# Depthwise convolutions on quarters of the array, and other rules for placing pieces, in a chain of four layers

## The chip, the cores and the metric

The kernel runs on one core of one Trainium2 chip. The metric is device time in microseconds (us), the median of several executions; lower is better. The engines are TensorE (PE, matrix products, with its weight loads shown as PEld), VectorE (DVE), ScalarE (ACT), GpSimd (POOL) and SyncE (SP), whose queue issues the transfers (DMA).

## What is computed

The input is x, 16 images of 192 channels and 32x32 pixels, in f32. Four layers follow each other: an mLSTM block with a 3x3 convolution and a batch norm over all images (layer 0); two attention blocks over channels with depthwise 3x3 convolutions (layer 1, of which the output needs the second attention with the first one's weights); a selective scan in four directions (layer 2); and a graph layer with sparse neighbours, a projection and a Gelu (layer 3). What the change touches is in layers 1 and 2:

```python
def dwconv3x3(x, w):
    return lax.conv_general_dilated(x, w, window_strides=(1, 1), padding='SAME', feature_group_count=x.shape[1], ...)
...
qkv = dwconv3x3(conv1x1(x, w_qkv), w_qkv_dw)
...
kvf = dwconv3x3(conv1x1(out, w_kv), w_kv_dw)
...
def step(h, xs_t):
    d_t, u_t, B_t, C_t = xs_t
    dA = jnp.exp(d_t[..., None] * A)
    h = h * dA + (d_t * u_t)[..., None] * B_t[:, :, None, :]
    y = jnp.einsum('bkdn,bkn->bkd', h, C_t)
    return (h, y)
```

In layer 2 an image has 384 inner channels, 16 states a channel, four directions and 1024 steps. Its depthwise convolution has 384 channels; those of layer 1 that the output needs have 384 (q and k), 192 (v) and 192 (the second v).

## The kernel before

Layer 0 runs over all images first and leaves its result in device memory. The rest is the class `LayersB`. Each image has three parts: `prepare` (layer 1 and the entry of layer 2), the scans of layer 2, and `complete` (the end of layer 2 and layer 3). While image b is scanned, `prepare(b + 1)` and `complete(b - 1)` run beside it as background streams. The first preparation and the last completion stand alone.

**The scans.** An image has 4 directions x 24 groups of 16 channels x 2 blocks of 8 states, 192 units (`UNITS`). One unit u is: `decay` (line 1830, ACT: h = exp(dl x A), 128x1024, into one of two PSUM buffers), `inputs` (line 1837, POOL: xs = du x bb, three buffers, two units ahead), `scan` (line 1844, DVE, in place in h), `outputs` (line 1849, DVE: hc = h x cb, three buffers), `sums` (line 1882, PE: four matmuls that add hc into the accumulator acc) and, each eighth unit, `collect` (line 1892, ACT copies acc to y). `fetch` loads dl, du, bb and cb on SP's queue. In directions 1 and 3 the sums read hc across (128 bytes from element to element).

**The projections.** `front(k)` makes dl and du of a direction, in six halves of 512 columns: `steps` (a matmul with dtw), `ends` (ACT: Abs and Relu), `logs` (ACT: Exp and Ln), `park` (POOL: dlh and duh, then two stores). `project` and `keep` do the same for the states, for two directions at once. Each piece has its unit written out by hand, with lags of 0, 1, 2 and 4 units.

**The background streams.** `prepare` and `complete` are generators. They yield the engine that their next piece needs. `scans` is a planner that runs when the program is built: it keeps a clock for each engine, adds to it what `Metered` puts down for each background instruction (`RATES`) and what a unit needs (`OWN`, `SLOT`), and lets a stream advance in a unit where `fits` says that the engine's clock lies less than `OVER` past the unit's end. `ALLOW` meters PE and DVE besides: 2.7 and 0.3 us of background work a unit. The instructions of each engine then stand in the order in which the planner issued them, and each engine takes its own in that order.

**Convolutions.** `conv` has ten calls an image: two for v and two for the second v (96 channels), three for q and k, three for layer 2 (128 channels). It takes the image padded to 34x34 from one of two pads, in two halves of 16 rows (512 columns), and for each half adds nine matmuls in one PSUM bank, each with a diagonal p x p weight matrix for its tap (from line 1140). An ACT copy takes each half away. `taps` loads the diagonal matrices from device memory, three taps a load; in the first image it makes them on DVE and stores them, and there DVE computes the second half of each convolution.

**PSUM.** Two tiles h of two banks each, acc of one, and one bank each for `prepare` ("bp"), `complete` ("bc") and `front` ("bf").

**Tables of ACT.** Gelu, Tanh and Ln with Exp need different function tables. `ln_exp` loads the one with Ln; a load is an instruction on ACT's queue. After each group of Gelu pieces the streams call `ln_exp`.

Nearly all background instructions have line 800, since `Metered` issues them.

Of the kernel before, what the change touches and what calls it, by code (L numbers as in the profile page):

```python
# [41 lines left out]
class Ctx:  # L42


    def __init__(self, tc, cpool, I):
        self.tc, self.nc, self.I = tc, tc.nc, I
        self.ordered = False
        self.has_ln = False
        nc = self.nc
        self.ident = cpool.tile([128, 128], F32, name="ident")  # L50
        nc.sync.dma_start(self.ident, I["c_ident"])
        self.blk6 = cpool.tile([P6, P6], F32, name="blk6")
        nc.sync.dma_start(self.blk6, I["c_blk6"])
        self.eps5 = cpool.tile([128, 1], F32, name="eps5")
        nc.vector.memset(self.eps5, 1e-5)
        self.one = cpool.tile([128, 1], F32, name="one")
        nc.vector.memset(self.one, 1.0)
        self.on192 = cpool.tile([P6, P6], F32, name="on192")
        nc.vector.memset(self.on192, 1.0 / C)
        self.on384 = cpool.tile([128, 128], F32, name="on384")  # L60
        nc.vector.memset(self.on384, 1.0 / INNER)
        self.ones = cpool.tile([128, 128], F32, name="ones")
        nc.vector.memset(self.ones, 1.0)

    def ln_exp(self):

        if self.ordered and self.has_ln:
            return
        self.has_ln = True
        if self.ordered:  # L70
            self.spent["ACT"] += TABLE
        i = self.nc.scalar.preload_act_table_set("natural_log_exp_and_others")
        if not self.ordered:
            self.tc.keep_in_program_order(i)
# [696 lines left out]
SLOT = 3.55  # L771
EARLY = 1.3
OWN = {"POOL": 2.36, "SUMS": 0.6, "START": 0.9, "DECAY": 1.1, "COLLECT": 0.57}
ENGINES = ("PE", "ACT", "POOL", "DVE")
ALLOW = {"PE": 2.7, "DVE": 0.3}
OVER = {"PE": 2.5, "ACT": 1.0, "POOL": 2.5}
LEAST = {"PE": 1.0, "ACT": 0.6, "POOL": 0.8}
# [3 lines left out]

class Metered:


    RATES = {"ACT": (0.07, 0.00105), "POOL": (0.1, 0.0022), "DVE": (0.08, 0.00105), "PE": (0.06, 0.0017)}
    LEAST = {"ACT": 0.2, "POOL": 0.2, "DVE": 0.12, "PE": 0.4}

# [3 lines left out]
    def __getattr__(self, op):  # L791
        f = getattr(self.engine, op)

        def issue(out, *args, **kw):
            base, each = self.RATES[self.name]
            self.spent[self.name] += max(self.LEAST[self.name], base + each * math.prod(out.shape[1:]))
            if op == "activation" and args[1] in (AF.Tanh, AF.Gelu):
                self.spent["ACT"] += TABLE * self.cx.has_ln
                self.cx.has_ln = False
            return f(out, *args, **kw)  # L800

        return issue
# [12 lines left out]
class Stream:  # L815
# [9 lines left out]
    def step(self):  # L825
        self.engine, lag, *mark = next(self.pieces, (None, 0))
        self.ready = self.at + lag
        self.piped = "piped" in mark

# [11 lines left out]
class LayersB:  # L841
# [10 lines left out]
    def mm(self):  # L852

        if self.bank is None:
            self.turn = (self.turn + 1) % 3
            tag = ("bp", "bc", "bf")[self.turn]
        else:
            tag = self.bank
        return self.mmp.tile([128, HL], F32, tag=tag, name="mm")

# [25 lines left out]
    def run(self):  # L886
        tc, NB = self.tc, self.NB
        self.bank, self.turn = None, 0
        with ExitStack() as ctx:
# [11 lines left out]
            self.parked = self.fetched = self.slots = self.scanned = self.read = 0  # L901

# [11 lines left out]
            with tc.manual_schedule():  # L914
                self.before, self.after = Stream(self.all(self.complete), "bc"), Stream(self.all(self.prepare), "bp")
                for b in range(NB):
# [6 lines left out]
    def setup(self):  # L923
# [3 lines left out]
        self.dqd = dp.tile([6, 128, 9, 128], F32, name="dqd")  # L927
        self.dvd = dp.tile([2, 2, P6, 9, P6], F32, name="dvd")
# [168 lines left out]
    def taps(self, p, src, w, first):  # L1097


        d = [self.slot("dg", [p, 3, p], "dg", 3) for _ in range(3)]  # L1100
        tv = None
# [3 lines left out]
        for t in range(3):  # L1105
            three = slice(3 * t, 3 * t + 3)
            if first:
                self.nc.vector.tensor_mul(
                    d[t], self.cx.ident[0:p, 0:p].unsqueeze(1).to_broadcast([p, 3, p]),
                    tv[:, three].unsqueeze(2).to_broadcast([p, 3, p]),  # L1110
                )
                self.nc.sync.dma_start(src[:, three, :], d[t])
            else:
                self.nc.sync.dma_start(d[t], src[:, three, :])
        return d, tv

    def conv(self, out, i, p, taps):


        nc = self.be  # L1120
        d, tv = taps
        for hf in range(2):
            if hf and tv is not None:
                yield "DVE", 0
                o = rows(out[:, half(hf)])
                for t in range(9):
                    v = self.pads[i][0:p, 16 + t // 3 : 32 + t // 3, t % 3 : t % 3 + W]
                    if t == 0:
                        nc.vector.tensor_scalar(o, v, tv[:, 0:1], None, op0=ALU.mult)
                    else:  # L1130
                        nc.vector.scalar_tensor_tensor(
                            o, v, tv[:, t : t + 1], o, op0=ALU.mult, op1=ALU.add
                        )
                continue
            yield "PE", 0
            ps = self.mm()[0:p, :]
            for t in range(9):
                if t in (2, 4, 6):
                    yield "PE", 0
                nc.tensor.matmul(  # L1140
                    ps, lhsT=d[t // 3][:, t % 3, :],
                    rhs=self.pads[i][0:p, 16 * hf + t // 3 : 16 * hf + t // 3 + 16, t % 3 : t % 3 + W],
                    start=(t == 0), stop=(t == 8),
                )
            yield "ACT", 0
            nc.scalar.copy(out[:, half(hf)], ps)

    def prepare(self, b):
# [193 lines left out]
        for g in range(3):  # L1342
            yield "ACT", 0
            nc.scalar.activation(xx[:, g, :], xg[:, g, :], AF.Gelu, bias=self.dw2b[:, g : g + 1])
        cx.ln_exp()
# [7 lines left out]
        for gs in ((0, 1), (2,)):  # L1353
# [10 lines left out]
            for g, z in zip(gs, zs):  # L1364
                yield "ACT", 0
                nc.scalar.activation(z, z, AF.Gelu)
                nc.sync.dma_start(self.zd[one(b), g].rearrange("o p l -> p (o l)"), z)
            cx.ln_exp()
# [5 lines left out]
    def complete(self, b):  # L1374
# [176 lines left out]
        for hf in range(2):  # L1551
# [57 lines left out]
            yield "ACT", 0  # L1609
            nc.scalar.activation(fin, fin, AF.Gelu)  # L1610
            cx.ln_exp()
# [22 lines left out]
    def scans(self, b, more, carry):  # L1634
# [4 lines left out]
        ahead = {}  # L1639
        for d in range(K + more):  # L1640
            for at, piece in self.front(d % K):
                if d % K or (at < 0) == (d > 0):
                    ahead.setdefault(d * DIR_UNITS + at, []).append(piece)
        for t in range(UNITS):
# [3 lines left out]
            for s in (self.before, self.after):  # L1648
                while s.engine == "ACT" and self.fits(s, now + EARLY - OVER["ACT"]):
                    self.advance(s)  # L1650
            if more or t + 1 < UNITS:
                self.decay((t + 1) % UNITS)
                clock["ACT"] += OWN["DECAY"]
# [4 lines left out]
            self.outputs(t)  # L1658
            clock["DVE"] += SLOT
            end = now + SLOT  # L1660
            if t > 0 or carry:
                self.sums((t - 1) % UNITS)
                self.collect((t - 1) % UNITS)
            self.fetch(t, more)
            self.bank = "bf"
            was = dict(self.spent)
            for piece in ahead.pop(t, ()):
                piece()
            for e in ENGINES:
                clock[e] += self.spent[e] - was[e]  # L1670
            for e in ALLOW:
                have[e] = min(have[e], 0.0) + ALLOW[e] - self.spent[e] + was[e]
            if more and t == FETCH:
                while self.parked < b + 2:
                    self.advance(self.after)
                self.fetch_xx()
            if t == UNITS - DIR_UNITS:
                while self.read < b:
                    self.advance(self.before)
            if t == 2:  # L1680
                self.scanned = b
            streams = (self.before, self.after)[:: 1 if t % 2 else -1]
# [6 lines left out]
        if not more:  # L1689
            while self.before.engine:  # L1690
                self.advance(self.before)
# [3 lines left out]
    def fits(self, s, end):  # L1695

        if not s.open(self.slots) or s.engine == "SP":
            return s.engine == "SP" and s.open(self.slots)
        at = self.clock[s.engine]
        if s.engine != "DVE":  # L1700
            end += OVER[s.engine]
        wait = s.inputs()
        if wait > at and (s.engine == "DVE" or wait + LEAST[s.engine] > end):
            return False
        return at < end + 0.1 and self.have.get(s.engine, 1.0) > 0.0

    def advance(self, stream):
        self.bank = stream.bank
        stream.at = self.slots
        was, wait = dict(self.spent), stream.inputs()  # L1710
        stream.step()
        for e in ENGINES:
# [7 lines left out]
    def begin(self):  # L1720

        for at, piece in self.front(0):
            if at < 0:
                piece()
# [12 lines left out]
    def front(self, k):  # L1737


# [48 lines left out]
        out = []  # L1788
        if k % 2 == 0:
            for hf in range(2):  # L1790
                at = -24 + 2 * hf
                out += [(at, lambda hf=hf: project(hf)), (at + 1, lambda hf=hf: keep(hf))]
        for n, at in enumerate((-18, -12, -6, 0, 6, 12)):
            for lag, f in ((0, steps), (1, ends), (2, logs), (4, park)):
                out.append((at + lag, lambda f=f, n=n: f(n // 2, n % 2)))
        return out
# [31 lines left out]
    def decay(self, u):  # L1828
        n, blk = divmod(u, BLOCKS)
        self.nc.scalar.activation(  # L1830
# [8 lines left out]
    def scan(self, u):  # L1839

        h, x = self.h[u % 2], self.xs[u % 3]
        if u // DIR_UNITS >= 2:
            h, x = h[:, ::-1], x[:, ::-1]
        self.nc.vector.tensor_tensor_scan(h, h, x, 0.0, op0=ALU.mult, op1=ALU.add)  # L1844
# [14 lines left out]
    def sums(self, u):  # L1859
# [5 lines left out]
        self.clock["PE"] += OWN["SUMS"]  # L1865
# [132 lines left out]
```

## Time and profile before

| | us |
|---|---|
| three runs | 15,191.56, 15,242.16, 15,250.05 |
| median | 15,242.16 |
| the profiled execution | 15,228.48 |
| its span, first to last instruction | 15,226.7 |

Busy time in the span, from the page:

| engine | busy us | share |
|---|---|---|
| PE | 12,507.7 | 82% |
| DVE | 12,530.6 | 82% |
| ACT | 7,798.3 | 51% |
| POOL | 10,305.3 | 68% |

The shares are means over stages with different limits. Up to about 3,090 us the span is layer 0, in which PE is busy 95% of the time and DVE under 50%. From there on the first preparation takes some 210 us, the scans of 16 images run from 3,300 to 15,079, and the last completion ends at 15,227.

The costliest groups have one line each in the page: instructions by line, engine and operation, what they write and read, the count, then busy us and mean ns of one. A scan (line 1844) takes 2,288 ns and its product (line 1849) 1,225 ns, 3,072 of each; a decay 1,116 ns; an xs 2,365 ns. A matmul in f32 leaves two records in the trace, one after the other. In the lists of waits a line names the waiting engine and tile, what ended the wait, and then the us in total, the times and the longest.

### The profile page before, as it was taken

To read this page: it belongs to the slowest core of one execution; us is meant where nothing else is said; L and a number is where in the kernel's file an instruction comes from. 1 tells how busy PE (TensorE), PEld (TensorE's weight loads), DVE (VectorE), ACT (ScalarE), POOL (GpSimd) and SP (SyncE) were. 2 spreads that over 40 slices of the span, in tenths; PEclk is the share of its full clock that TensorE was granted. 3 is DMA by queue.
4 is the path that set the end of the run, shared out by engine and by line. 5 is a ranking of instruction groups with operands and counts; after the bars stand their busy time and mean duration, and the time that the engine had idled before them with its cause. 6 is when DMAs were issued, how large, how long until landed. Compare 5 with 4: busy or idle time off the path is not lost. (4 is left out here: it accounts for less than half of the span.)

```text
span 15226.7 us, 183204 instructions
## 1 busy us (share of the span) xinstructions
PE 12507.7 (82%) x65856; PEld 4757.9 (31%) x65856; DVE 12530.6 (82%) x10115; ACT 7798.3 (51%) x10376; POOL 10305.3 (68%) x6314
## 2 busy tenths in 40 slices
PE   8999999978787778788887878788887888787655
PEld 4444444422232222222222222222222222222212
DVE  4444444459899999999999899999999999989997
ACT  3333333334555556465646565655555555555554
POOL 2222222227687878787878787878888787878785
PEclk9999999978888888888888888888888878888766
DMA  1000000047778787878777778777777787777775
GB/s 29 15 15 15 15 15 15 15 109 192 202 195 212 188 209 193 209 196 204 195 201 200 195 199 199 202 196 204 196 199 201 203 197 204 193 205 195 198 181 128
DMA packets 884772, 2412.01 MB, mean 158 GB/s; under 512 B 146672, under 2 KB 266944, under 8 KB 876224
## 3 DMA queue, kind: packets, MB, share of 16 engines
q1 hardware_dynamic: 871168, 2397.50, 62.2%
q8 instruction: 532, 8.72, 0.3%
q10 hardware_dynamic: 12736, 3.04, 0.1%
q14 instruction: 336, 2.75, 0.1%
HBM read 2019.10 MB, written 364.30 MB: 157 GB/s over the span
## 5 line engine op out<-in xcount | busy, mean ns | idle before, releaser
L1837 POOL TENSOR_TENSOR xs<-du,bb 128x1024 f32<-128x1024 f32 x3072 | 7236.2, 2365 | 1967.3 <-DVE h L1844 1511.0
L1844 DVE TENSOR_TENSOR_SCAN h<-h,xs 128x1024 f32<-128x1024 f32 x3072 | 7028.1, 2288 | 440.3 <-ACT h L1830 391.4
L1830 ACT ACTIVATE h<-dl,A 128x1024 f32<-128x1024 f32 x3072 | 3424.6, 1116 | 3605.1 <-DVE hc L1849 3066.4
L1882 PE MATMUL acc<-hc,sel 128*32 128x256 f32 x24576 | 2741.8, 527 | 1651.5 <-DVE hc L1849 1640.5
L1849 DVE TENSOR_TENSOR hc<-h,cb 128x1024 f32<-128x1024 f32 x3072 | 3761.9, 1225 | 363.3 <-PE acc L1882 53.0
L800 PE MATMUL mm<-pad,dg 128*128 128x512 f32 (+1 forms) x5580 | 2791.1, 637 | 152.1 <-DMA dg<-dqd 39.0
L627 POOL TENSOR_TENSOR D<-D,mask 128x256 f32<-128x256 f32 x768 | 543.4, 740 | 2100.1 <-DVE D L624 2100.1
L1882 PEld LDWEIGHTS acc<-hc,sel 128*32 128x32 f32 x24576 | 549.8, 118 | 3958.7 <-DVE hc L1849 2717.5
L800 PEld LDWEIGHTS mm<-pad,dg 128*128 128x128 f32 (+1 forms) x5580 | 970.4, 187 | 1682.2 <-issue 1399.8
L800 PE MATMUL mm<-x,wgt 96*128 96x512 f32 (+1 forms) x1664 | 1067.3, 775 | 148.9 <-ACT o L800 43.2
L800 POOL TENSOR_TENSOR t<-x 96x768 f32<-96x768 f32 (+4 forms) x510 | 650.8, 1298 | 79.5 <-ACT x L800 47.8
L800 PE MATMUL mm<-d,xT 128*96 128x256 f32 x2048 | 588.5, 428 | 15.8 <-POOL d L800 13.3
L800 PE MATMUL mm<-xd,dtw 12*128 12x512 f32 x768 | 559.1, 815 | 8.0 <-ACT z L800 8.0
L800 POOL TENSOR_TENSOR duh<-dlh,xx 128x512 f32<-128x512 f32 x384 | 538.3, 1402 | 30.1
L800 POOL TENSOR_TENSOR dlh<-dlh,e 128x512 f32<-128x512 f32 x384 | 488.4, 1272 | 103.7 <-ACT e L800 101.8
L800 PEld LDWEIGHTS mm<-x,wgt 96*128 96x128 f32 (+1 forms) x1664 | 335.4, 223 | 697.1 <-issue 339.9
L391 PE MATMUL pc<-ypad,w_c 128*64 128x512 f32 (+1 forms) x1152 | 480.2, 664 | 74.4 <-PEq L751 41.6
L1892 ACT COPY y<-acc 128x512 f32<-128x512 f32 x384 | 224.6, 585 | 543.3 <-PE acc L1882 539.2
L624 DVE SCALAR_TENSOR_TENSOR D<-D,s 128x256 f32<-128x256 f32 x768 | 271.6, 415 | 255.3 <-ACT D L620 255.3
L1870 PE MATMUL acc<-y,ident 128*128 128x512 f32 x576 | 387.7, 761 | 84.9 <-ACT y L1892 84.9
L800 PEld LDWEIGHTS mm<-d,xT 128*96 128x96 f32 x2048 | 340.2, 179 | 321.2 <-issue 131.6
L620 ACT ACTIVATE D<-s 128x256 f32<-128x256 f32 x768 | 233.3, 389 | 337.9 <-PE s L613 332.4
(321 smaller groups left out, 14230.1 us busy)
## 6 DMA issues: line engine op xcount, KB each, us to landing
dl<-dld SPq DMA_DIRECT2D x1536, 512.0 KB
du<-dud SPq DMA_DIRECT2D x1536, 512.0 KB
dld<-dlh SPq DMA_DIRECT2D x384, 256.0 KB
dud<-duh SPq DMA_DIRECT2D x384, 256.0 KB
bb<-xdr SPq DMA_DIRECT2D x128, 512.0 KB
cb<-xdr SPq DMA_DIRECT2D x128, 512.0 KB
dg<-dqd SPq DMA_DIRECT2D x270, 192.0 KB
zd<-z SPq DMA_DIRECT2D x48, 512.0 KB
```

Source lines behind the costliest of these rows:

```text
L391: nc.tensor.matmul(p[r, :], lhsT=w_, rhs=v, start=(n == 0), stop=(n == 14))
L620: nc.scalar.activation(d, S[j][:, two], AF.Exp)
L624: nc.vector.scalar_tensor_tensor(d, d, 2.0, S[j][:, 2 * CH :], op0=ALU.min, op1=ALU.mult)
L627: nc.gpsimd.tensor_mul(d, d, mask)
L800: return f(out, *args, **kw)
L1830: self.nc.scalar.activation(self.h[u % 2], self.dl[n % 2], AF.Exp, scale=self.A[:, blk, n : n + 1])
L1837: self.nc.gpsimd.tensor_mul(self.xs[u % 3], self.du[n % 3], self.turn_of(self.bb, n // GROUPS, blk))
L1844: self.nc.vector.tensor_tensor_scan(h, h, x, 0.0, op0=ALU.mult, op1=ALU.add)
L1849: self.nc.vector.tensor_mul(self.hc[u % 3], self.h[u % 2], self.turn_of(self.cb, k, at % BLOCKS))
L1870: nc.tensor.matmul(acc, lhsT=self.cx.ident, rhs=self.y[:, g, half(pair)], start=True, stop=False)
L1882: nc.tensor.matmul(self.acc[rows4(q), q4(s)], lhsT=self.sel[:, m, :], rhs=part(q), start=False, stop=(s + m + blk == 3),)
L1892: self.nc.scalar.copy(y, self.acc)
```

## The change

It has five parts.

1. Convolutions: each tap is four matmuls. Channels 0 to 63 and the rest are two row blocks, the two halves of the image two column blocks; a row block has its own PSUM bank ("bf" is taken besides the stream's own, `mm2`). The weights are 64 columns wide, one load for nine taps, two buffers. For 96 channels the second block is 32 rows by 32 columns. The planner adds `TAP` for each tap. Four ACT copies of 64x512 (or 32x512) take the result away. The DVE path of the first image goes.
2. Projections: `front` becomes a generator, `fronts`, and a third stream with the first claim. Its pieces have an earliest unit and a latest one, at which `force` issues them.
3. A lock: who is to use "bf" says "take" and "give"; the other waits between.
4. Gelu pieces are marked; they are issued where they end by the plan 1.2 us ahead of the unit's end, and the next decay loads the table with Ln back.
5. The planner's figures change. PE isn't metered any more, background DVE pieces may stand between a scan and its product, and PE is held to 1.0 us past the unit's end ahead of each eighth unit. A function `pooled`, which is False for every unit, has branches of its own; none of them is taken.

```diff
-SLOT = 3.55
+SCAN, PRODUCT = 2.29, 1.34
 EARLY = 1.3
-OWN = {"POOL": 2.36, "SUMS": 0.6, "START": 0.9, "DECAY": 1.1, "COLLECT": 0.57}
+OWN = {"POOL": 2.37, "SUMS": 0.8, "TURNED": 1.05, "START": 1.25, "DECAY": 1.12, "COLLECT": 0.59}
+TAP = 1.2
-ALLOW = {"PE": 2.7, "DVE": 0.3}
+ALLOW = {"DVE": 0.45}
 OVER = {"PE": 2.5, "ACT": 1.0, "POOL": 2.5}
+SOON = {"PE": 1.0, "ACT": 0.0, "POOL": 1.0}
+GELU = 1.2
...
+def pooled(u):
+    return False
...
-    RATES = {"ACT": (0.07, 0.00105), "POOL": (0.1, 0.0022), "DVE": (0.08, 0.00105), "PE": (0.06, 0.0017)}
+    RATES = {"ACT": (0.07, 0.00105), "POOL": (0.1, 0.0022), "DVE": (0.14, 0.00105), "PE": (0.06, 0.0019)}
...
     def taps(self, p, src, w, first):
-        d = [self.slot("dg", [p, 3, p], "dg", 3) for _ in range(3)]
+        d = self.slot("dg", [p, 9, 64], "dg", 2)
...
+    def conv(self, out, i, p, d):
+        nc = self.nc
+        blocks = [slice(0, 64), slice(64, p)]
+        yield "PE", 0, "take"
+        banks = [self.mm(), self.mm2()]
+        for t in range(9):
+            if t in (2, 4, 6):
+                yield "PE", 0
+            for r, ps in zip(blocks, banks):
+                n = r.stop - r.start
+                for hf in range(2):
+                    nc.tensor.matmul(
+                        ps[64 * hf : 64 * hf + n, :], lhsT=d[r, t, 0:n],
+                        rhs=self.pads[i][r, 16 * hf + t // 3 : 16 * hf + t // 3 + 16, t % 3 : t % 3 + W],
+                        start=(t == 0), stop=(t == 8),
+                    )
+            self.spent["PE"] += TAP
+        for r, ps, mark in zip(blocks, banks, ("", "give")):
+            yield "ACT", 0, mark
+            for hf in range(2):
+                self.be.scalar.copy(out[r, half(hf)], ps[64 * hf : 64 * hf + r.stop - r.start, :])
...
-            yield "ACT", 0
+            yield "ACT", 0, "gelu"
             nc.scalar.activation(xx[:, g, :], xg[:, g, :], AF.Gelu, bias=self.dw2b[:, g : g + 1])
-        cx.ln_exp()
...
+            if t % 8 == 7:
+                over["PE"] = SOON["PE"]
...
+            for s in (self.front, self.before, self.after):
+                while s.engine == "ACT" and not pooled(t) and self.fits(s, now + EARLY - over["ACT"]):
                     self.advance(s)
...
             self.scan(t)
-            self.outputs(t)
-            clock["DVE"] += SLOT
+            clock["DVE"] += SCAN
+            if not pooled(t):
+                for s in (self.before, self.after):
+                    while s.engine == "DVE" and self.fits(s, clock["DVE"]):
+                        self.advance(s)
+                self.outputs(t)
+                clock["DVE"] += PRODUCT
...
+            while self.ended < 2 * ((b * K * GROUPS + min(n + 3, ends - 1)) // 8 + 1):
+                self.force(self.front)
...
+        if s.take and self.lock not in (None, s):
+            return False
         at = self.clock[s.engine]
+        wait = s.inputs()
+        if s.gelu:
+            return self.quiet and max(at, wait) < end - GELU
...
+    def force(self, stream):
+        while stream.take and self.lock not in (None, stream):
+            self.advance(self.lock)
+        self.advance(stream)
...
+        for n in range(6):
+            while self.slots < at - 18 + 6 * n:
+                yield "SP", 1
+            yield "PE", 0, "take"
+            steps(n // 2, n % 2)
+            yield "ACT", 0, "give"
+            ends(n // 2, n % 2)
+            yield "ACT", 0
+            logs(n // 2, n % 2)
+            yield "POOL", 0
+            park(n // 2, n % 2)
+            self.ended += 1
...
     def decay(self, u):
+        if self.cx.ordered:
+            was = self.spent["ACT"]
+            if self.cx.table == "gelu":
+                self.cx.ln_exp()
+            self.clock["ACT"] += OWN["DECAY"] + self.spent["ACT"] - was
```

## The prediction

> **What bounds the kernel now.** I read the windows by stage first, then the waits of VectorE (DVE) and of ScalarE (ACT), then the groups by shape, then TensorE (PE) in order of time. All sums below are made against the profiled execution, 15,228.5 us with a span of 15,226.7; it lies 14 us under the median of the three runs, 15,242, so a figure made here is raised by 14 us where it is set beside that median.
>
> The windows cut the run into layer 0's end with the first image's preparation, the scans of images 1 to 14, the scans of image 15, and the tail. (The scans of image 0 take another 738 us, 3300 to 4038.)
> ```profile
> core 0: us, PE busy (x) PEld busy (x) DVE busy (x) ACT busy (x) POOL busy (x), PEclk, DMA share, GB/s
> 3090.00:3300.00 210.00, 159.51 (x418) 71.11 (x415) 97.16 (x192) 66.76 (x109) 11.98 (x9) 0.87 0.28 72
> ...
> 4038.00:14381.00 10343.00, 8406.89 (x38051) 2876.46 (x38049) 9590.61 (x6286) 5811.60 (x7166) 8406.92 (x4676) 0.83 0.79 200
> 14381.00:15079.00 698.00, 384.78 (x2120) 115.00 (x2120) 669.60 (x411) 346.87 (x391) 589.64 (x327) 0.61 0.75 187
> 15079.00:15227.00 148.00, 100.28 (x422) 47.25 (x422) 56.73 (x85) 57.33 (x80) 25.14 (x42) 0.73 0.11 34
> ```
> The reader is to see that DVE is the bound of every scan stage: 9590.6 of 10,343 us, 685 of 739 us an image. Its idle time is 53.7 us an image. Image 15, which has no next image to prepare, has the same 192 units and only 28.4 us idle. So what better placing of the other engines' work can win is 53.7 - 28.4 = 25.3 us for each of 14 images, 354 us, and about 10 us in image 0 (41 us idle above 28.4, of which 31.6 is one wait at its start). The floor is some 14,865 us; no edit here takes an instruction off DVE inside the scans.
>
> The waits of DVE, of ACT, and the groups by shape of the scan stages:
> ```profile
> DVE h L1844 <- ACT h L1830: 391.4, 273, 8.1
> DVE hc L1849 <- PE acc L1882: 53.0, 40, 3.0
> DVE yh L800 <- PE mm L800: 50.1, 15, 5.2
> DVE h L1844 <- POOL xs L1837: 39.5, 7, 31.6
> ...
> ACT y L1892 <- PE acc L1882: 532.0, 210, 9.8
> ACT h L1830 <- DMA dl<-dld: 515.7, 150, 8.4
> ACT pad L800 <- PE mm L800: 307.9, 167, 3.8
> ```
> ```profile
> L800 PE MATMUL mm<-pad,dg 128*128 128x512 f32 x3240 | 1603.2, 629 | 102.2 <-DMA dg<-dqd 39.0 <-ACT xg L800 22.2 <-ACT e L800 15.1
> L800 PE MATMUL mm<-pad,dg 96*96 96x512 f32 x2160 | 1109.0, 652 | 49.8 <-ACT v L800 28.3 <-DMA dg<-dvd 15.8 <-ACT vf L800 3.0
> L800 ACT ACT_TABLE_LOAD x212 | 272.0, 1283 | 3.8
> ```
> A scan waits for its decay (391 us), and the decay stands in ACT's queue behind a copy that waits for PE, above all the copy of the accumulator (210 of 383 wait, 532 us). I followed each late scan back along ACT's records to the instruction that ended ACT's last idle time. About 150 us of the 391 start at an accumulator copy, 118 at a Gelu with its table loads (z 48, fin 30, xg 40), some 70 at other copies that wait for PE, the rest at the decay itself, which waited for its input.
>
> **The change, part by part.**
>
> *Convolutions on PE.* Ten convolutions an image, six of 128 channels and four of 96. Before: 18 matmuls each, two records a matmul, (1603.2 + 1109.0)/5400 = 0.502 us a record, so 18.1 us each and 181 us of the 601 PE-busy us an image. After: 36 matmuls on quarters of the array, four to a tap. Layer 0 shows quarters side by side:
> ```profile
> 568.27 2.36 PE L391 MATMUL pc<-ypad,w_c2p 64*64 64x512 f32 x10
> ...
> 1500.42 1.03 PE L391 MATMUL pc<-ypad,w_c 128*64 128x512 f32 x4
> 1501.38 0.73 PE L613 MATMUL s<-at,itg 32*128 32x128 f32 x16
> ```
> Ten records of 512 columns in 2.36 us are five pairs of 0.43 us. For 128 channels all four tiles have one size: 18 waves x 0.502 = 9.0 us. For 96 channels the second block is 32x32, so sizes alternate inside each tap. No row shows unlike tiles side by side. Bounds: all four together, 9.0 us, or each pair alone, 36 waves x 0.502 = 18.1 us plus 18 changes of size at 0.10 us (the second timeline line starts at 1501.38, where two waves of 0.43 after 1500.42 would give 1501.28), 19.9 us. I take the upper, because every change of size in layer 0 shows that gap. PE then needs 6 x 9.0 + 4 x 19.9 = 134 us, 47 less an image: 554 of 739 us, 75% for 81%.
>
> [...]
>
> Fewer busy PE records can also lower the granted clock: 0.83 at 81% busy, 0.61 in image 15 at 55%. There the records of the sums took 573 ns for 522, so 10% is the price: 554 becomes at most 609 us an image, still under 739. It is hidden. [...]
>
> *Evacuation.* Four copies of 512 columns a convolution for two: 20 more an image at 0.587 us (the row of pad copies of that size), 11.7 us on ACT, 415 to 427 of 739. Hidden by ACT's idle time; bare, 11.7 x 14 = 164 us.
>
> *PE's lateness.* The planner's own figures rise from 0.93 to 1.03 us a matmul (the trace: 1.00), from 0.6 to 0.8 or 1.05 for the sums, and PE is held back ahead of each collection. In the built program's order I counted the other matmuls that stand between the last two sums ahead of each of the 384 accumulator copies: at least 2 us of them in 223 cases before, in 77 after. So the 150 us fall by two thirds, -100 (bounds -150 and 0). The 70 us at other copies, 53 at hc and 50 at yh also wait for PE; PE's busy share above image 15's 55% falls from 26 to 20 points, and its plan is nearer the trace: I take a little under half off, -80 (bounds -150 and 0).
>
> *Gelu by the next decay.* Same pieces, and as many table loads in that order (434 for 423), but a Gelu is placed only where its table's return fits ahead of the decay. Half of 118: -60 (bounds -118 and 0).
>
> *Projections as a third stream.* The same 2.7 us of Abs, Relu, Exp and Ln now often stand in one gap between decays. Gaps with more than 3.8 us of ACT work (its records' durations in the built order) rise from 247 to 440, their excess from 365 to 542 us. Behind them wait the next decay and so the scan. At the rate of the Gelu gaps, 118 of 365, this costs 57 us; with inputs that are ready by plan, nothing. I take +25. GpSimd's (POOL) work is the same 9.6 ms, but its excess over 3.8 us a unit in stretches of eight rises from 152 to 448 us; each us is counted in up to eight stretches, so at least 296/8 = 37 us is real, and xs has two units in hand: +15 (0 to 37).
>
> *96-channel convolutions against their plan.* The plan counts 9 x 1.2 = 10.8 us; at 19.9 PE runs 9.1 late. Queued behind are the sums and the convolution's copies, behind those on ACT the next decay, and for that the scan. A decay has a unit's length, 3.8 us, less its own 1.12, so 2.7 us in hand; the nearly empty PE gaps around the convolution in the built order give back some 5. Left 1 to 2: 60 convolutions x 1.3 = +80 (0 to 60 x 6.4 = 384, nothing given back).
>
> *Diagonal weights.* Half the bytes and one load for three (450 issues to 150 on SP's queue, which the loads of dl and du share): the 55 us that PE waited for dg go, but these lie beside DVE. Nothing, unless a late dl is behind it. DVE pieces put between a scan and its product delay the sums and the next scan alike: nothing.
>
> *First image.* DVE did half of each convolution, 7 us of each, beside PE; PE now does all: 6 x 7.7 + 4 x 17.3 us (unthrottled waves of 0.43) = 116 for 77 us in a window where PE is busy 160 of 210: +15 (-10 to 39). The tail has no convolution: 0.
>
> Sum: -100 - 80 - 60 + 25 + 15 + 80 + 15 = -105, so 15,123 on the profiled execution and 15,137 beside the median; I say 15,130.
>
> **Rivals.** (a) *The unlike tiles overlap after all.* For it: the mixed rows of layer 0 compete for the same strips, ours do not. Against: the 0.10 us gap at every change. Then +80 goes, +15 becomes -10 and PE is at 69%, which takes some 40 more off its waits: -250, 14,990. (b) *Slower: the 96-channel convolutions hold ACT.* PE late by 9 us, two in a row at the start of a preparation and two in its middle, and each time the copies block the decay. For it: a blocked accumulator copy already cost up to 9.8 us. Against: PE has 25% idle. Without this term the sum is -185, so it decides from 185/60 = 3.1 us a convolution and tells as slower from 4.4 us; at the full 6.4, +384 - 185 = +199, about 15,440; with 5.5, 15,390. (c) *The waits only move.* DVE must wait for ACT as long in the crowded gaps as it did at the accumulator: -100 - 80 - 60 against 57 + 37 + 150, 15,245.
>
> **How the numbers follow.** The forecast 0.40, (a) 0.20, (b) 0.26, (c) 0.14. What a measurement here can tell from no change is about 0.5%, 76 us. The forecast spreads over its bounds, 15,020 to 15,210, and a fifth of it falls within 0.5% (0.08); (a) is faster; (c) within, of which I give a third to each side. Faster 0.32 + 0.20 + 0.05 = 0.57, same 0.08 + 0.04 + 0.03 of (b) = 0.15, slower 0.28. The range reaches over (a) to 14,920 and into (b) to 15,400; the forecast's own is 15,020 to 15,210.
>
> **What would show it.** Records of the 96-channel convolutions in pairs 0.43 us apart and not in fours: the serial bound; in fours: (a). The wait of y for acc should fall from 532 to under 200 us, that of h for its decay from 391 to some 240, and DVE's idle time an image from 53.7 to about 46. Were h's wait for its decay above 391 with v and vf copies ahead of it in ACT's queue, (b) holds. The forecast is wrong if DVE's busy time an image moves from 685 us, or if scans wait for xs by more than 80 us.

## The result, and the profile after

| | before | after |
|---|---|---|
| median | 15,246.1 us (4 runs) | 16,194.5 us (4 runs) |
| lowest to highest | 15,191.6 to 15,275.3 | 16,177.9 to 16,250.8 |
| span of the profiled execution | 15,226.7 | 16,249.0 |

The ratio is 1.0633 [1.0592, 1.0674]: the change makes the kernel 6.3% slower, 948 us by the medians and 1,022 by the two profiled spans. The time lies 794 us above the range. The windows by stage of the kernel after, cut where its stages end (the columns are those of the prediction's first fence):

```profile
core 0: us, PE busy (x) PEld busy (x) DVE busy (x) ACT busy (x) POOL busy (x), PEclk, DMA share, GB/s
3090.00:3420.00 330.00, 272.30 (x980) 85.27 (x976) 36.41 (x92) 87.54 (x143) 12.26 (x10) 0.74 0.17 44
3420.00:4300.00 880.00, 652.13 (x2915) 161.04 (x2916) 668.29 (x431) 438.92 (x525) 519.38 (x244) 0.65 0.64 163
4300.00:15400.00 11100.00, 8546.81 (x42868) 2545.64 (x42870) 9585.18 (x6287) 5925.07 (x7403) 8402.46 (x4678) 0.74 0.72 183
15400.00:16100.00 700.00, 380.57 (x2120) 113.31 (x2117) 669.74 (x411) 344.13 (x389) 588.62 (x326) 0.62 0.74 185
```

DVE's busy time in images 1 to 14 is what it was, 9585.18 for 9590.61 us, 685 an image. Its idle time an image went from 53.7 to 108 us. The stage is 757 us longer, the scans of image 0 142, the first preparation 120; image 15, which prepares nothing, takes 700 for 698, and the tail 149 for 148. So everything that was lost was lost where convolutions run. PE's busy time there rose (8546.81 for 8406.89), though it was to fall by 47 us an image, and the granted clock fell from 0.83 to 0.74.

What DVE waited for, and below it ACT (us in total, times, longest):

```profile
DVE hc L1918 <- PE acc L1951: 800.0, 107, 16.3
DVE h L1907 <- ACT h L1892: 439.5, 257, 12.7
...
DVE dg L1127 <- PE mm L1150: 207.1, 8, 41.1
DVE h L1907 <- POOL xs L1899: 129.7, 94, 57.4
```
```profile
ACT h L1892 <- DMA dl<-dld: 952.5, 231, 10.9
ACT v L813 <- PE mm L1150: 474.7, 58, 28.0
ACT vf L813 <- PE mm L1150: 454.9, 64, 30.7
...
ACT y L1961 <- PE acc L1951: 313.6, 82, 22.9
```

The product hc waits for a free buffer, that is for the sums on PE: 800 us for 53. It is 107 waits of 7.5 us. ACT waits for v and vf, the results of the four 96-channel convolutions. The wait for dg is in the first preparation, where DVE makes weights in two buffers and PE is slow to release them. The convolutions by shape in the kernel after:

```profile
L1150 PE MATMUL mm<-pad,dg 64*64 64x512 f32 x9216 | 1854.6, 701 | 31.5 <-ACT pad L813 16.3 <-ACT dlh L813 12.0 <-DMA dg<-dvd 2.2
L1150 PE MATMUL mm<-pad,dg 32*32 32x512 f32 x2304 | 979.8, 943 | 6.6 <-ACT dlh L813 6.6
```

Together 2,834 us. The two shapes of before were, over the same whole span:

```profile
L800 PE MATMUL mm<-pad,dg 128*128 128x512 f32 x3348 | 1650.6, 628 | 102.4 <-DMA dg<-dqd 39.0 <-ACT xg L800 22.2 <-ACT e L800 15.1
L800 PE MATMUL mm<-pad,dg 96*96 96x512 f32 x2232 | 1140.4, 650 | 49.8 <-ACT v L800 28.3 <-DMA dg<-dvd 15.8 <-ACT vf L800 3.0
```

Quarters of the array saved nothing. The 32x32 matmuls, a fifth of the count, take 943 ns each and a third of the time.

One such convolution, the v at 8,129 us: PE in order of time, then DVE (start, us, instructions, in brackets the idle time before), then the windows with PE's busy time and its clock (the third window holds four taps, the fourth three).

```profile
8129.12 4.04 PE L1150 MATMUL mm<-pad,dg 64*64 64x512 f32 x16
8133.09 1.05 PE L1951 MATMUL acc<-hc,sel 128*32 128x256 f32 x8
8134.06 15.06 PE L1150 MATMUL mm<-pad,dg 64*64 64x512 f32 x32
8149.05 2.08 PE L1939 MATMUL acc<-y,ident 128*128 128x512 f32 x2
8151.06 1.08 PE L1951 MATMUL acc<-hc,sel 128*32 128x256 f32 x8
8152.07 11.31 PE L1150 MATMUL mm<-pad,dg 64*64 64x512 f32 x24
```
```profile
8141.30 2.29 DVE L1907 TENSOR_TENSOR_SCAN h<-h,xs 128x1024 f32<-128x1024 f32 x1
8152.21 1.22 DVE L1918 TENSOR_TENSOR hc<-h,cb 128x1024 f32<-128x1024 f32 x1 [8.62 <-PE acc L1951]
```
```profile
8120.00:8129.00 9.00, 6.15 (x38) 1.41 (x30) 8.79 (x6) 8.57 (x10) 8.74 (x6) 1.00 0.86 205
8129.00:8134.00 5.00, 5.00 (x28) 0.82 (x24) 4.79 (x4) 2.90 (x5) 4.92 (x4) 0.94 0.96 245
8134.00:8149.00 15.00, 15.00 (x36) 1.89 (x32) 9.38 (x6) 3.84 (x4) 11.42 (x5) 0.50 0.67 178
8152.00:8163.00 11.00, 11.00 (x28) 1.42 (x24) 3.43 (x2) 1.16 (x2) 2.34 (x1) 0.50 0.00 0
```

The first two taps take 2.0 us each. In the next window the clock is at 0.50, and a tap takes 3.75 us. PE is busy in every one of those 15 microseconds, and in the 9 ahead of the convolution, at clock 1.00, it was busy for 6.15. So it is not idleness that halves the clock here. Over all 64 such convolutions the matmuls of one take 29.4 us of PE's time in the mean, 34.0 from the first to the last with the sums that stand between, where the plan counts 10.8. The sums of the units stand behind them in PE's order, the three buffers of hc fill, and DVE waits 8.62 us.

### The profile page after: what moved, and what is told of

It is laid out like the page before. It is cut to its first block, busy times and chain, and to the rows that moved or that the text cites. A ratio compares the mean times of both kernels' runs of the same rounds, so it can differ in the third digit from the quotient of the medians.

```text
span 16249.0 us, 194242 instructions
## 1 busy us (share of the span) xinstructions
PE 12855.8 (79%) x71796; PEld 4428.4 (27%) x71796; DVE 12463.6 (77%) x10015; ACT 7992.9 (49%) x10713; POOL 10296.8 (63%) x6314
## 5 line engine op out<-in xcount | busy, mean ns | idle before, releaser
L1951 PE MATMUL acc<-hc,sel 128*32 128x256 f32 x24576 | 2844.4, 555 | 2016.4 <-DVE hc L1918 2011.4
L1150 PE MATMUL mm<-pad,dg 64*64 64x512 f32 (+1 forms) x11520 | 2768.5, 749 | 38.2 <-ACT dlh L813 18.6
L1951 PEld LDWEIGHTS acc<-hc,sel 128*32 128x32 f32 x24576 | 606.9, 125 | 4321.3 <-DVE hc L1918 3331.9
L813 PE MATMUL mm<-x,wgt 96*128 96x512 f32 (+1 forms) x1664 | 1009.3, 741 | 103.6 <-ACT pad L813 58.3
L1150 PEld LDWEIGHTS mm<-pad,dg 64*64 64x64 f32 (+1 forms) x11520 | 502.0, 143 | 2079.5 <-issue 1912.3
L813 PE MATMUL mm<-xd,dtw 12*128 12x512 f32 x768 | 597.8, 868 | 168.2 <-ACT qk L813 102.8
L813 PE MATMUL mm<-d,xT 128*96 128x256 f32 x2048 | 626.2, 447 | 120.7 <-POOL d L813 110.7
L1939 PE MATMUL acc<-y,ident 128*128 128x512 f32 x576 | 464.7, 900 | 78.9 <-ACT y L1961 78.6
L813 ACT ACTIVATE e<-mm,v_dt_b 128x512 f32<-128x512 f32 x384 | 261.3, 680 | 304.3 <-PE mm L813 286.8
```

Of the source, the lines that this page charges most:

```text
L1150: nc.tensor.matmul(ps[64 * hf : 64 * hf + n, :], lhsT=d[r, t, 0:n], rhs=self.pads[i][r, 16 * hf + t // 3 : 16 * hf + t // 3 + 16, t % 3 : ...
L1939: nc.tensor.matmul(acc, lhsT=self.cx.ident, rhs=self.y[:, g, half(pair)], start=True, stop=False)
L1951: nc.tensor.matmul(self.acc[rows4(q), q4(s)], lhsT=self.sel[:, m, :], rhs=part(q), start=False, stop=(s + m + blk == 3),)
```

## The experiments

Three causes could lie behind the loss. The 96-channel convolutions cost the time because their small tiles run at half clock; or because they are longer than the plan's 10.8 us, at any clock; or the loss is in the other rules, the crowded projections, the Gelu or the hold of PE. No kernel here leaves work out.

**The 96-channel convolutions whole again** (`e1_whole96`; the 128-channel ones stay but for their weights, which come in two loads, and so do all rules; the plan prices these convolutions at some 18.6 us, so the order of the pieces moves).

```diff
+        if p < 128:
+            for hf in range(2):
+                ...
+                    nc.tensor.matmul(
+                        ps, lhsT=d[t // 3][:, t % 3, :],
+                        rhs=self.pads[i][0:p, 16 * hf + t // 3 : 16 * hf + t // 3 + 16, t % 3 : t % 3 + W],
...
```

> The four 96-channel convolutions of an image go back to 18 whole 96x96 matmuls each; all else is as in the changed kernel. Theory (their half-filled waves bring the clock to half, 34 us each against 10.8 in the plan, and the sums stand behind them): the waits of hc for the sums go from 800 us to under 80, 15,000 to 15,150 us. Rival (the new placing of pieces costs the time, whatever the convolutions): above 15,800 us.

Measured: 15,177 us, 0.9959 [0.9944, 0.9974]. The wait of hc for acc is 7.6 us, and the time lies 27 us above what was expected. So the loss goes with these four convolutions; as the order of the pieces moves too, it takes the next run to clear the other rules.

**Their second block filled to 64x64 with zero weights** (`e2_pad64`; every instruction stands where it did but for four more clears on DVE in the first image, the same number of matmuls with the same 512 columns; rows 96 to 127 of the pad meet weights of zero).

```diff
-        d = self.slot("dg", [p, 9, 64], "dg", 2)
+        d = self.slot("dg", [128, 9, 64], "dg", 2)
         if first:
+            if p < 128:
+                self.nc.vector.memset(d[p:128], 0.0)
...
-        blocks = [slice(0, 64), slice(64, p)]
+        blocks = [slice(0, 64), slice(64, 128)]
```

> The second block of the 96-channel convolutions is filled up to 64x64 with zero weights, so that all four tiles of a tap have one size and run together. Theory: waves of four 0.43 to 0.47 us apart, 8.4 us a convolution, full clock, 14,850 to 15,000 us, the fastest of these. Rival (new placing costs the time): above 15,800 us. Second rival (any quarter tile halves the clock): waves 0.85 us apart for 96 channels, 15,300 us or more.

Measured: 15,135 us, 0.9927 [0.9910, 0.9943], 1,059 us less than the kernel after, though 135 more than the upper end expected. Of its profile the convolutions by shape, and a wait of DVE and one of ACT:

```profile
L1152 PE MATMUL mm<-pad,dg 64*64 64x512 f32 x11520 | 1491.6, 630 | 38.3 <-ACT dlh L813 17.4 <-ACT pad L813 16.1 <-DMA dg<-dvd 4.1
```
```profile
DVE h L1909 <- ACT h L1894: 317.8, 215, 10.6
DVE h L1909 <- POOL xs L1901: 133.3, 99, 60.9
```
```profile
ACT h L1894 <- DMA dl<-dld: 968.2, 231, 10.3
ACT y L1963 <- PE acc L1953: 106.7, 64, 7.1
```

There is more arithmetic, a quarter of those convolutions' rows on zeros, and the busy time of all convolutions is nearly halved, 2,834 to 1,492 us. Four tiles of one size run together, and a tap is 0.94 us (two waves of 0.468). This removes the serial pairs and the half clock at once, so both of the first two causes still stand. With the order unchanged, the other rules fall as the cause. The clock holds in these convolutions although a quarter of the rows meet weights of zero: 6% of all waves of fours are at half clock, for 5% of those of the kernel after, whose fours have no such rows.

**Pairs of one size, and two sizes apart.** `e6_pairs` takes the filled blocks, but the first block's nine taps and then the second's, so that only two tiles run at a time. `e3_apart` does this with the blocks of the change, 64x64 and then 32x32: as many waves as the change, one change of size for 17. In the traces of these two, of `e2_pad64` and of the kernel after, every engine takes its instructions behind layer 0 in the same order, but for the clears named above and the order of the taps within these convolutions. So their times differ by the tiles alone.

```diff
+        turns = [(t, (0, 1)) for t in range(9)]
+        if p < 128:
+            turns = [(t, (0,)) for t in range(9)] + [(t, (1,)) for t in range(9)]
...
-            self.spent["PE"] += TAP
+            self.spent["PE"] += TAP * len(which) / 2
```

> As e2_pad64, but for 96 channels the nine taps of the first block run ahead of the nine of the second: pairs of 64x64 tiles only, half the array filled all the time, no change of size. If the array's filling sets the clock: a share of half-clock waves between that of fours (5%) and that of 32x32 pairs (55% in e3_apart), 0.55 to 0.65 us a wave, 15,400 to 15,650 us. If small tiles or changes of size do: waves of 0.45 to 0.50 us and 15,250 us or less.

> The 96-channel convolutions do nine taps of the 64x64 pair first and then nine taps of the 32x32 pair: the same matmuls, one change of size for 18. If the alternation of sizes brings the clock down: records 0.43 us apart, 15.5 us a convolution, about 15,300 us. If it is the array's filling (two of four quarters, or two of sixteen): records 0.85 us apart after some 4 us, 31 us a convolution, 15,900 to 16,100 us.

Measured: `e6_pairs` 15,396 us, 1.0095 [1.0075, 1.0116]; `e3_apart` 15,730, 1.0319 [1.0296, 1.0342]. The waits of hc, first of `e6_pairs` and then of `e3_apart`:

```profile
DVE hc L1924 <- PE acc L1957: 158.3, 56, 13.1
```
```profile
DVE hc L1922 <- PE acc L1955: 385.3, 80, 14.5
```

From the starts of the matmul records I took the step from one wave (tiles that start together) to the next, in us, and the share of steps at half clock, which lie near 0.9 us:

```
kernel       wave                         median  mean   at half clock
after        four 64x64 (128 channels)    0.429   0.465    5%
e2_pad64     four 64x64 (all)             0.429   0.468    6%
e6_pairs     64x64 pair to 64x64 pair     0.429   0.506   21%
e3_apart     64x64 pair to 64x64 pair     0.430   0.577   31%
e3_apart     32x32 pair to 32x32 pair     0.739   0.647   50%
after        64x64 pair to 64x64 pair     0.907   0.771   66%
after        64x64 pair to 32x32 pair     0.994   0.866   72%
after        32x32 pair to 32x32 pair     0.852   0.744   71%
after        32x32 pair to 64x64 pair     0.992   0.868   74%
```

This is a ladder of three steps. The matmuls of one 96-channel convolution take 9.2, 17.6, 22.4 and 29.4 us of PE's time in `e2_pad64`, `e6_pairs`, `e3_apart` and the kernel after (over all records, also of tiles that don't start together). Two tiles at a time for four, `e2_pad64` to `e6_pairs`: +260 us. That is mostly the length against the plan, 17.6 us for 10.8, with a little of the clock in it. A second block of 32x32 for 64x64, to `e3_apart`: +334, the clock alone, since at full clock both sizes step by 0.43. The two sizes in turn for one after the other, to the kernel after: +465, of which the 17 changes of size, at 0.09 us each, are some 64 x 1.5 = 98; the rest is the clock. So by this estimate the half clock is some 700 of the 1,059 us. `e3_apart` lies between its two expectations (about 15,300, and 15,900 to 16,100): neither the turns nor the small tiles alone are the whole of it. `e6_pairs` comes near the lower end of its first (15,400).

What brings the clock down can be read from its records, which have 1.00 or 0.50 for whole windows of 3.41 us (in the kernels before and after, each record but the last is a whole number of them long). For every window of all fourteen profiles (layer 0, the same in all, included) I added up the rows and columns of the tile times the streamed columns (512 in a wave) of its matmuls, as a share of the whole 128x128 array in use (a wave of 512 columns in 0.853 us at half clock, the commonest step there between 128x128 matmuls of 512 columns, and in half of that, 0.427, at full clock, where the commonest step is 0.429), and looked at the clock of the next window:

```
share of    at full clock         at half clock
the array   windows  full next    windows  full next
under 0.2     3,445         15      3,091          0
0.2 to 0.3    2,252        657      8,929          0
0.3 to 0.4    2,803      2,317      2,484          0
0.4 to 0.5    3,619      3,619      2,534          1
0.5 to 0.8   16,476     16,476      7,835      2,922
over 0.8      8,706      8,706      2,574      2,574
```

PE's busy time does not sort the windows so. At full clock, 864 with PE busy for under 70% and a share of 0.4 or more all stayed there; of 89 with PE busy for 97% or more and a share under 0.25, 83 fell. Four 64x64 tiles fill windows to 0.9 and more, a pair of 64x64 to 0.5, a pair of 32x32 to 0.13, and the two pairs in turn to 0.23 to 0.31. So a pair of 64x64 mostly keeps the clock that it finds: of the windows that hold nothing else, in `e6_pairs` and `e3_apart`, all 100 at full clock stayed and 20 of 142 at half rose. A pair of 32x32 loses it (20 of 20 fell in `e3_apart`) and so do the two in turn (43 of 43 in the kernel after), and neither gets it back (0 of 104, 0 of 334). `e3_apart` is faster than the change because its first nine taps keep a full clock where they find one. All matmuls here are f32, and the bounds are no finer than the rows.

**The plan told the true length** (`e4_honest`, `+= TAP if p == 128 else 3.75`), and **all ten convolutions whole under the new rules** (`e5_allwhole`).

> The plan counts 3.75 us a tap of 96 channels, as measured, for 1.2; the instructions are the same and only their order moves. If the lateness against the plan is what costs: hc's waits for the sums fall from 800 us to under 200 and the time to 15,300 to 15,500 us. If PE's capacity at the low clock is what costs: no fall, above 15,950 us.

> All ten convolutions of an image are 18 whole matmuls again; the third stream, the lock, the Gelu rule and the plan's figures stay as in the changed kernel. If the rules alone bring what e2_pad64 gained (0.7%): 15,100 to 15,200 us. If the gain came from the shorter convolutions of 128 channels: 15,250 us or more, as PE is back at 80% in the scans.

Measured: 19,307 us, 1.2665 [1.2639, 1.2692], and 18,659, 1.2235 [1.2214, 1.2255]. Waits of DVE in `e4_honest`:

```profile
DVE h L1907 <- ACT h L1892: 1536.0, 351, 58.2
DVE x L813 <- PE mm L813: 1513.5, 85, 93.6
DVE yh L813 <- PE mm L813: 926.8, 13, 80.0
```

Neither kernel was expected to do this. By its own figures, added up over the program, the planner then puts some 654 us and 639 us on PE in an image of 192 x 3.63 = 697, where the change has 562. In the traces the scans stand still behind units 144 and 161 of an image (of 192), 3,670 us in all in `e4_honest` and 3,221 in `e5_allwhole`. These are the two units at which the code forces what is left of `complete` and of `prepare`, and there x and yh wait up to 93.6 us. So the streams have fallen behind, and their leftovers stand alone. An honest price alone doesn't help where the plan has no room for it, and the new rules by themselves can't carry the whole convolutions.

**A queue behind its stores** (`e7_store_later`, on `e2_pad64`: the stores of dl and du two units later).

```diff
             park(n // 2, n % 2)
+            yield "SP", 2
+            store(n // 2, n % 2)
```

> As e2_pad64, but the two stores of a projection stand two units later on SP's queue than GpSimd's products. Theory (the stores wait for GpSimd at the head of the queue, 1,634 us for 305 before the change, and the loads of dl behind them are late): SP's waits for dlh under 400 us, ACT's waits for dl from 968 to under 600 us, 14,990 to 15,080 us. Rival (the loads of dl are late because the memory is busy): SP's waits fall, ACT's for dl stay above 850 us, 15,120 us or more.

`e2_pad64` has a wait that was small before. SP's queue, before and in `e2_pad64`:

```profile
SPq L1785 <- POOL dlh L800: 310.5, 131, 4.7
```
```profile
SPq L1832 <- POOL dlh L813: 1634.3, 294, 13.1
```

The store of dl stands ahead of the loads in SP's order and waits for POOL; the decay's wait for dl went from 515.7 to 968.2 us. With the stores later that wait of SP is 167.8 and ACT's wait for dl is 654.5, but the scans' wait for their decay is 417.3 instead of 317.8 and the time 15,237, 0.9991 [0.9982, 1.0001], 102 us more and not the 55 to 145 less that were expected. The order of the other pieces moves with the stores. So this wait is not what `e2_pad64` still loses, or the cure costs more than it gives; which is open.

**Single rules**, all on the filled tiles with `TAP = 0.95`, near the 0.94 us that a tap takes (`e8_tap`). `e9_no_hold` drops `over["PE"] = SOON["PE"]`; `e10_old_gelu` issues the Gelu as before, with `ln_exp` after each group; `e11_no_between` keeps DVE pieces from standing between a scan and its product; `e12_both` joins the ninth and the tenth.

> As e2_pad64, with the plan's cost of a tap at 0.95 us, the measured pace of two waves, for 1.2. If the plan's surplus leaves PE idle and delays the streams: 15,060 to 15,110 us. If it only moves pieces: within 0.3% of e2_pad64, 15,090 to 15,180 us.

> As e8_tap (15,117 us), without the rule that holds PE back ahead of each eighth unit. If that rule is what took the accumulator's waits away, as my term of -100 us says: ACT's waits of y for acc from 152 to over 350 us and 15,190 to 15,240 us. If the lighter convolutions did it: under 250 us and within 0.3% of e8_tap.

> As e8_tap, with the Gelu pieces placed as before the change, and the table with Ln loaded back right behind them. If the Gelu rule is worth my term of -60 us: 15,160 to 15,200 us, with late scans behind z, xg and fin of over 100 us. If a Gelu costs the same in either place: within 0.3% of e8_tap.

> As e8_tap, with no background piece of DVE between a scan and its product. My forecast put this at nothing: within 0.3% of e8_tap, 15,070 to 15,165 us. Rival (the earlier pieces shorten the streams' chains): 15,200 us or more.

> Filled tiles with tap 0.95 (15,117 us), and both rules undone: no hold of PE ahead of each eighth unit (alone 15,074) and the Gelu placed as before (alone 15,053). If the two rules cost separately, the gains of 0.28 and 0.42% of before add up: 15,000 to 15,030 us. If both only free the same order of pieces on ACT and PE, no more than the better of the two: 15,040 to 15,080 us.

| | us | ratio to before | scans wait for decays, us | y waits for acc, us |
|---|---|---|---|---|
| `e8_tap` | 15,117 | 0.9912 [0.9896, 0.9929] | 327 | 152 |
| `e9_no_hold` | 15,074 | 0.9884 [0.9867, 0.9900] | 297 | 310 |
| `e10_old_gelu` | 15,053 | 0.9874 [0.9857, 0.9890] | 267 | 182 |
| `e11_no_between` | 15,153 | 0.9937 [0.9920, 0.9953] | 334 | 198 |
| `e12_both` | 15,143 | 0.9941 [0.9927, 0.9955] | 364 | 381 |

`e8_tap` and `e11_no_between` came out at their expectation of no effect, within 0.3%; `e9_no_hold` gave the time of one expectation with a wait between the two, and `e10_old_gelu` and `e12_both` met neither of theirs. The hold or the Gelu rule undone alone makes the kernel faster, both undone make it slower than either and no faster than with both: the old Gelu placing gives 64 us with the hold and takes 69 without it (58 and 87 by the ratios to the kernel before, which ran beside each). Each edit moves the pieces behind it: of PE's 71,796 records about a third stand elsewhere than in `e8_tap`. So a rule has no price of its own here, and `e11_no_between`'s 36 us are no proof for that rule. `e10_old_gelu` beats both kernels, by 1.3% the one before.

## Why the prediction was wrong

**The step that failed** is "96-channel convolutions against their plan", with its line "10% is the price", "It is hidden". The convolution was priced at 19.9 us and took 29.4, spread over 34. The serial pairs and the gap at a change of size were right: where the clock is full, the steps of a tap have medians of 0.481 + 0.525 + 0.454 + 0.523 = 1.98 us, 18 us a convolution. What was missed is the clock. The price of a lower clock was taken from the sums in image 15, 573 for 522 ns, as a mean over a stage. But the clock records of the trace hold only 1.00 and 0.50, and the clock fell in these convolutions, after every window at full clock that they filled (43 of 43): no mean over a stage shows what one burst pays. The spare time of PE, 25% in the mean, was no cover either: the three buffers of hc are full after three units, 11 us, and the sums stand in PE's order behind pieces like that of 15 us above.

The term itself, +80 with bounds 0 and 384, is measured by the ladder. From the starts of the scans:

```
               before   after   e6_pairs  e2_pad64  e10_old_gelu
first scan us    3311    3426      3349      3330      3331
image 0, us       738     886       803       756       725
images 1 to 14, mean  738.7  792.7  743.6     729.4     725.1
```

Beside the scans, after against `e2_pad64`, it is 14 x 63.3 + 130 = 1,016 us over 60 convolutions, 17 us each. At less than the forecast's own length (`e6_pairs`, 17.6 us) it is 14 x 14.2 + 47 = 246, 4.1 us each where I had left 1.3, and past the 3.1 from which rival (b) decides. Of 6.8 us late only 2.7 were given back, where the prediction counted on 2.7 and some 5. So the term was too small even with little of the clock in it; with all of it, it left its bounds.

**Rival (b)** named the place and the sign, but its price had the same cap and its road was half wrong: the copies of v and vf did block ACT (475 and 455 us), yet the scans' wait for the decay rose only from 391 to 440. DVE was stopped by PE itself, through hc. PE was busy for 15.00 of 15.00 us at 0.50, and by the table of windows the clock went with the share of the array in use: at half clock all 2,574 windows with 0.8 or more rose, and one of 17,038 with under 0.5. The prediction had read the clock from PE's busy share, with image 15, whose rows held none of the new tiles.

**Right.** DVE bounds the scans, at 685 us busy an image. The 128-channel convolutions: 18 x 0.465 = 8.4 us for 9.0. Unlike tiles did not overlap, so rival (a) fell: unlike pairs start one after the other, at full clock 0.52 us apart in the kernel after, where like ones start 0.43 apart in `e3_apart`.

**Right only in sum.** With the four convolutions cured, the change gives 15,135, and I had said 15,130. That the two figures meet is luck: I had charged 80 us for these convolutions, and the other terms do not stand as I set them.
- *The accumulator's copy*, -100: y's wait for acc went from 532 to 314 with the slow convolutions and to 107 in `e2_pad64`. The wait fell as forecast. But `e9_no_hold` has twice the wait of `e8_tap` and is faster, so the wait is no measure of the time.
- *PE's lateness elsewhere*, -80: DVE's waits for it fell in `e2_pad64`, hc for acc from 53 us to nothing and yh from 50 to 12, and its idle time an image is some 45 us there, for 46 forecast; in the kernel after hc waits 800. What this alone is worth was not tried, nor the +25 for the third stream.
- *Gelu by the next decay*, -60: +64 or -69, as the rest of the plan falls. The whole wait of scans for decays, 391 to 318 in `e2_pad64`, is 74 us, half of the 160 and more that the two terms together had claimed.
- *POOL bursts*, +15 (0 to 37): the wait for xs without its longest was 8 us and is 72. In all it is 130 us in the kernel after, above the 80 that were named as a sign against the forecast. That the bursts cause it was not tried.
- *SP's queue*, nothing: in `e2_pad64` that queue stood 1,634 us for POOL. I had looked at the loads that went, and not at what the stores wait for once projections stand close together.
- *First image*, +15 (-10 to 39): the first scan comes 115 us later in the kernel after, since nothing covers the slow convolutions there, and 19 in `e2_pad64`, within the bounds.

## What to carry to other kernels

Part-filled tiles had a price beyond their waves here, by the estimate above some 700 us for the half clock: look at the clock inside the burst, not at a stage's mean, and work out which share of the array each window of a burst will use. If a split leaves blocks of unlike size, try to fill the small ones with zeros to the size of the others, which won 1,059 us here. A planner's figure for one instruction group must be right for a burst, since the queue behind it may have buffers for a few units only; here the three of hc were full after 11 us. And where a planner places everything, price a rule only by runs of several plans; here undoing either of two rules gained 0.3 to 0.4%, and undoing both gained nothing.

## Not expected of the hardware

- PE busy all the time ran at clock 0.50 through 15 and 11 us while it worked with pairs of 64x64 and 32x32 tiles in turn; four 64x64 tiles together ran at 0.43 us a wave in `e2_pad64`, 94% of them at full clock, also where a quarter of the rows met zero weights. Over 14 profiles all 28,801 windows at full clock with a share of the array of 0.4 or more kept it, 864 with PE busy for under 70% among them, 3,430 of 3,445 with under 0.2 lost it, one of 17,038 at half clock with under 0.5 got it back, and all 2,574 with 0.8 or more did.
- A change between 64x64 and 32x32 tiles cost 0.09 us at full clock (0.52 in the kernel after for 0.43 in `e3_apart`; 0.04 to 0.07 beside the like pairs of the kernel after, 0.48 and 0.45) and 0.09 to 0.14 at half (0.994 for 0.907 or 0.852, medians of the kernel after), though the tiles share no rows and no bank.
